# The MLP of a conditioned transformer block: both products as seven block products in place of eight, in groups of 512 tokens, with the first of them among the last steps of cross-attention

## The chip, the cores and the metric

The kernel runs on one core of one Trainium2 chip. The metric is the device time of one execution in microseconds (us), the median of several runs. All arithmetic that matters here is in float32.

## The reference

The block takes 16 images of 224 tokens with 512 channels (3584 tokens), one conditioning vector per image, and 750 context tokens per image. Cut to what matters:

```python
shift_a, scale_a, gate_a, shift_m, scale_m, gate_m = split(silu(c) @ W_mod + b_mod, 6)
x = x + gate_a * proj(self_attention(ln(x) * (1 + scale_a) + shift_a))     # 16 heads of 32
x = x + cproj(cross_attention(ln(x), ln(context)))
x_norm2 = ln(x) * (1 + scale_m) + shift_m
h = gelu(x_norm2 @ W_mlp1 + b_mlp1)        # 512 -> 2048
x = x + gate_m * (h @ W_mlp2 + b_mlp2)     # 2048 -> 512
```

The change is about the last two lines, and about the step that leads into them.

## The kernel before

Three stages follow each other: self-attention in pairs of images, cross-attention image by image, and the MLP. Every instruction is kept in program order on its engine (class `Ordered`, line 19), so the code's order is the order of each queue; since all calls go through that helper, the profile puts them on line 28, and groups are told apart by their tiles.

**A float32 product on TensorE.** A call of `mm` with a stationary block of 128 x 128 and a moving block of 128 x n stands in the profile as two matmul instructions and two weight loads (LDWEIGHTS, shown as engine PEld): each pass streams the n columns once. A transpose (`turn`) is one pass. The text calls one such instruction a *pass*.

**Cross-attention** (from line 698). It goes by units, one for each image b and group g of four heads. `plan` and `at_slot` (line 791) hang the other work of the image (projections, transposes, norms) into six slots of each unit. A unit's `scores` go to the PSUM tile `sc` (four banks, one buffer); VectorE (DVE) keeps a running maximum `top`; ScalarE (ACT) copies the scores to `pt`; one unit later `max_row`, `subtract` (DVE, tile `pt`) and `weights` (exponentials on ACT, the row sums `acc` on GpSimd, POOL) follow, and `values` multiplies with `vt` and adds the sums of `acc` (tile `o`); `finish` divides (DVE, `rinv` and `at`). `project` (line 773) multiplies the heads' results `at` by `wcproj`, adds them to the image `x` (DVE `upd`, then POOL) and writes the image to `x_cross` in DRAM. After the last unit comes a tail written out by hand (lines 993 to 1014): the last unit's weights and values, with four products of the MLP set between them (`ahead`), and the last image's `project`.

**The MLP** (from line 1018) takes four groups of 896 tokens. For a group, `mlp_load` fetches a chunk of 128 tokens (tile `mx`), `mlp_norm` normalises it (statistics on DVE, the rest on POOL), `mlp_turn` transposes it on TensorE and modulates it on DVE into `mxt`. For the first group these steps are hung into the slots of the last image of cross-attention (lines 828 to 837), all seven chunks of them. The first product (`mlp_1`, line 684) makes 128 of the 2048 rows of `h` for 448 tokens from four calls, eight passes of 448 columns; ACT applies the GELU (`h`). The second product then makes 128 tokens x 512 channels from 16 calls, 32 passes of 512 columns; DVE adds the bias (`upd`), POOL multiplies by the gate and adds the image, and the rows go out. While it runs, the next group is loaded, normalised and turned. The four weight blocks of each product are loaded by SyncE's queue (SP), those of the second when the memory of cross-attention has come free.

Of the kernel before, what the change touches and what calls it, by code (L numbers as in the profile page):

```python
# [8 lines left out]
F32 = mybir.dt.float32  # L9
# [28 lines left out]
def kernel(  # L38
# [44 lines left out]
    NG = B // GB  # L83
    GT = GB * N
    GC = GT // P
    HT = GT // 2
    NT = 3
# [64 lines left out]
    x_cross = [dram.tile([GT, H], F32, name=f"x_cross{q}") for q in range(NG)]  # L152
# [269 lines left out]
    def load_cross():  # L422

        mod_pool.close()
        p = cross_weights.enter_context(tc.tile_pool(name="w_cross", bufs=1, side="right"))
# [215 lines left out]

    mlp_in = ExitStack()
    mlp = {}
    mx = {}

    def mlp_begin():
        context_pools.close()
        p = mlp_in.enter_context(tc.tile_pool(name="ml_in", bufs=1, side="right", reuse_waits="tile"))
        mlp["in"] = p
        mlp["w1"] = []  # L650
        mlp_weights(2)

    def mlp_weights(n):
        for i in range(len(mlp["w1"]), n):
            mlp["w1"].append(load_w(mlp["in"], w_mlp1[:, i * H : (i + 1) * H], f"w1_{i}"))

    def mlp_load(i):
        q, c = divmod(i, GC)
        mx[i] = cw["mx"].tile([P, H], F32, name="mx")
        nc.sync.dma_start(out=mx[i], in_=x_cross[q][c * P : (c + 1) * P, :])  # L660

    def mlp_norm(i):
        Norm([mx[i]], [mx[i]], P).all()

    def mlp_turn(psum, i):
        q, c = divmod(i, GC)
        if c == 0:
            mlp["xt"] = [mlp["in"].tile([P, GT], F32, name=f"mxt{k}") for k in range(KC)]
# [4 lines left out]
        lo, hi = c * P, (c + 1) * P  # L673
        while lo < hi:
            b = lo // N
            to = min((b + 1) * N, hi)
            for k in range(KC):
                at = (k - c) * P
                modulate(
                    ps[:, at + lo : at + to], mlp["xt"][k][:, lo:to], q * GB + b, k, i_shift_m, i_scale_m  # L680
                )
            lo = to

    def mlp_1(ps, m, half):
        w, lo = mlp["w1"][m // KC], (m % KC) * P
        for k in range(KC):
            mm(
                ps[:, :HT], w[:, k, lo : lo + P], mlp["xt"][k][:, half * HT : (half + 1) * HT],
                start=(k == 0), stop=(k == KC - 1),
            )  # L690
# [4 lines left out]
    with tc.tile_pool(name="ca", bufs=2, reuse_waits="tile") as ca:  # L695
# [98 lines left out]
        for b in range(B):  # L794
# [30 lines left out]
            if n == B:  # L825
# [6 lines left out]
                at_slot(b, 3, 0, lambda: mlp_weights(MLP // H))  # L832
                for c, (u, slot) in enumerate(((2, 3), (2, 4), (2, 5), (3, 0), (3, 1), (3, 2), (3, 4))):
                    at_slot(b, u, slot, lambda c=c: mlp_turn(ps_mm, c))
                    if 4 + c < GC:
                        at_slot(b, u, slot, lambda c=c: mlp_load(4 + c))
                        at_slot(b, *((2, 5), (3, 0), (3, 1))[c], lambda c=c: mlp_norm(4 + c))
# [155 lines left out]
        early = {}  # L993
        sc = ps_s.tile([P, HG, 512], F32, name="sc")

        def ahead(m):
            early[m, 0] = sc[:, m, :]
            mlp_1(early[m, 0], m, 0)
# [8 lines left out]
        ahead(2)  # L1007
# [10 lines left out]
    with tc.tile_pool(name="ml", bufs=3, reuse_waits="tile") as ml:  # L1018
        hs = {}

        def gelu(ps, m, half):
            if half == 0:
                hs[m] = ml.tile([P, GT], F32, name="h", bufs=NF + 1)
            nc.scalar.activation(
                hs[m][:, half * HT : (half + 1) * HT], ps[:, :HT], AF.Gelu_apprx_tanh,
                bias=bcol[:, o_mlp + m : o_mlp + m + 1],
            )

        for (m, half), ps in early.items():
            gelu(ps, m, half)  # L1030
        attention_psum.close()

        w2 = [load_w(ml, w_mlp2[i * H : (i + 1) * H, :], f"w2_{i}") for i in range(MLP // H)]
        bmlp2 = bias_rows(ml, b_mlp2, P, "bmlp2")
        resid = {}

        def fetch(i):
            if i < NG * GC:
                q, c = divmod(i, GC)
                t = ml.tile([P, H], F32, name="xr")  # L1040
                nc.sync.dma_start(out=t, in_=x_cross[q][c * P : (c + 1) * P, :])
                resid[i] = t, gate_rows(ml, 1, i * P, P)

        fetch(0)
        fetch(1)
        with (
            tc.tile_pool(name="ml_h", bufs=4, space=PSUM, reuse_waits="tile") as ps_h,
            tc.tile_pool(name="ml_mm", bufs=4, space=PSUM, reuse_waits="tile") as ps_mm,
        ):
            for q in range(NG):  # L1050
                for m in range(NF):
                    for half in range(2):
                        if q or (m, half) not in early:
                            ps = ps_h.tile([P, 512], F32, name="h_ps")
                            mlp_1(ps, m, half)
                            gelu(ps, m, half)
                more = q + 1 < NG
                if more:
                    mlp_load((q + 1) * GC)
                    mlp_load((q + 1) * GC + 1)  # L1060
                for c in range(GC):
                    i = q * GC + c
                    if more:
                        if c + 2 < GC:
                            mlp_load(i + GC + 2)
                        mlp_norm(i + GC)
                    ps = ps_mm.tile([P, 512], F32, name="mm")
                    for m in range(NF):
                        mm(
                            ps[:, :H], hs[m][:, c * P : (c + 1) * P], w2[m // KC][:, m % KC, :],  # L1070
                            start=(m == 0), stop=(m == NF - 1),
                        )
                    fetch(i + 2)
                    if more:
                        mlp_turn(ps_mm, i + GC)
                    x_r, gate = resid.pop(i)
                    add_to_x(ml, ps[:, :H], x_r, bmlp2, gate)
                    nc.sync.dma_start(out=out.flatten_outer_dims()[i * P : (i + 1) * P, :], in_=x_r)
# [36 lines left out]
```

## Time and profile before

| what | value |
|---|---|
| median of 3 runs | 3063.89 us (3062.92 to 3065.47) |
| the profiled execution's own time | 3062.88 us |
| its span in the profile | 3061.1 us |
| TensorE busy | 2965.4 us, 97% of the span |
| DVE, ACT, POOL busy | 1618.5, 1129.1, 1251.9 us |
| granted TensorE clock, mean | 0.99 |
| last image's units end, `project` of it begins | 2267.51 us |
| first matmul of the MLP after that | 2285.06 us |
| last matmul ends, last instruction of POOL begins | 3054.64, 3056.85 us |

The time outside of the span is 1.8 us. In a row of the timeline the first number is the start, the second the length of a run of like instructions, "x8" their number, and a bracket at the end the idle time before them with what ended it. Ends of matmuls are modelled: in a row of passes the next begins before the last one's modelled end, so the pace is read from starts.

### The profile page before, as it was taken

To read this page: it belongs to the slowest core of one execution; us is meant where nothing else is said; L and a number is where in the kernel's file an instruction comes from. 1 tells how busy PE (TensorE), PEld (TensorE's weight loads), DVE (VectorE), ACT (ScalarE), POOL (GpSimd) and SP (SyncE) were. 2 spreads that over 40 slices of the span, in tenths; PEclk is the share of its full clock that TensorE was granted. 3 is DMA by queue.
4 is the path that set the end of the run, shared out by engine and by line. 5 is a ranking of instruction groups with operands and counts; after the bars stand their busy time and mean duration, and the time that the engine had idled before them with its cause. 6 is when DMAs were issued, how large, how long until landed. Compare 5 with 4: busy or idle time off the path is not lost.

```text
span 3061.1 us, 44601 instructions
## 1 busy us (share of the span) xinstructions
PE 2965.4 (97%) x18709; PEld 1622.0 (53%) x18709; DVE 1618.5 (53%) x2294; ACT 1129.1 (37%) x1316; POOL 1251.9 (41%) x1624
## 2 busy tenths in 40 slices
PE   8999999998999999999999999999869999999999
PEld 5554454454556555555555655655535444454444
DVE  3555555564577777777777787777740100201100
ACT  1122222221465656656656566566522011020110
POOL 1022222122366766666766766676640210202101
PEclk9999999999999999999999999999989999999999
DMA  5111110101101000001000101100220110201001
GB/s 182 56 31 31 31 31 17 51 10 31 49 27 33 25 23 30 30 26 33 33 23 21 33 23 33 33 23 1 79 91 18 56 41 14 83 0 55 31 11 41
DMA packets 55373, 114.28 MB, mean 37 GB/s; under 512 B 4308, under 2 KB 4372, under 8 KB 55172
## 3 DMA queue, kind: packets, MB, share of 16 engines
q1 hardware_dynamic: 54560, 110.58, 11.2%
q8 instruction: 147, 2.41, 0.3%
q10 hardware_dynamic: 612, 0.85, 0.1%
q14 instruction: 54, 0.44, 0.0%
HBM read 89.33 MB, written 22.09 MB: 36 GB/s over the span
## 4 chain that ended last, share of the span: by engine, by line
PE 73%; issue 12%; DVE 7%; POOL 4%; ACT 3%; DMA 1%; POOLq 0%; ACTq 0%; SPq 0%; DVEq 0%
PE mm L28 50%; PE sc L28 9%; PE o L28 8%; PE h_ps L28 6%; ACT pt L28 3%; DVE top L28 2%; POOL acc L28 1%; DVE rinv L28 1%; DVE stats L28 1%; POOL upd L28 1%; POOL xr L28 1%; DVE mc L28 1%; DVE m L28 1%; ACT kt L28 0%; DVE pt L28 0%
## 5 line engine op out<-in xcount | busy, mean ns | idle before, releaser
L28 POOL TENSOR_TENSOR acc<-acc,pt 125x448 f32<-125x448 f32 x512 | 583.5, 1140 | 40.2
L28 POOL TENSOR_TENSOR upd<-upd,gate 112x512 f32<-112x512 f32 (+1 forms) x60 | 76.1, 1269 | 1124.7 <-DVE upd L28 1120.0
L28 DVE TENSOR_TENSOR pt<-pt,o 125x896 f32<-125x896 f32 x384 | 394.4, 1082 | 91.1 <-PE o L28 86.1
L28 ACT COPY pt<-sc 125x1792 f32<-125x1792 f32 x192 | 317.4, 1653 | 225.7 <-DVE top L28 201.3
L28 PE MATMUL mm<-w,h 128*128 128x512 f32 x896 | 388.2, 592 | 0.0
L28 PE MATMUL h_ps<-mxt,w 128*128 128x448 f32 x992 | 376.3, 542 | 9.2 <-ACT h L28 9.2
L28 DVE TENSOR_TENSOR top<-top,sc 125x896 f32<-125x896 f32 x320 | 346.7, 1083 | 40.6 <-PE sc L28 34.0
L28 PE MATMUL mm<-wkvc,cxt 128*125 128x512 f32 x768 | 354.4, 604 | 8.6 <-ACT kt L28 8.6
L28 PE MATMUL mm<-cxt,wkvc 128*128 128x375 f32 x1024 | 349.9, 484 | 2.5 <-ACT cxt L28 2.5
L28 ACT ACTIVATE pt<-pt 125x896 f32<-125x896 f32 x384 | 339.3, 955 | 14.5 <-DVE pt L28 13.7
L28 DVE TENSOR_SCALAR mxt<-mm,mod_t 128x128 f32<-128x128 f32 (+3 forms) x160 | 47.0, 362 | 510.3 <-PE mm L28 510.3
L28 POOL TENSOR_TENSOR acc<-pt 125x448 f32<-125x448 f32 x128 | 146.2, 1142 | 375.1 <-ACT pt L28 375.1
L28 ACT ACTIVATE h<-h_ps,bcol 128x448 f32<-128x448 f32 x124 | 78.6, 634 | 595.6 <-PE h_ps L28 595.6
L28 PEld LDWEIGHTS h_ps<-mxt,w 128*128 128x128 f32 x992 | 189.3, 191 | 194.4 <-issue 184.4
L28 PEld LDWEIGHTS mm<-w,h 128*128 128x128 f32 x896 | 168.8, 190 | 205.3 <-issue 205.3
L28 DVE RECIPROCAL rinv<-o 128x224 f32<-128x224 f32 x128 | 198.8, 1553 | 115.5 <-PE o L28 115.5
L28 PEld LDWEIGHTS mm<-cxt,wkvc 128*128 128x128 f32 x1024 | 190.1, 191 | 112.6 <-issue 12.9
L28 ACT ACTIVATE pt<-sc 112x1792 f32<-112x1792 f32 x64 | 106.5, 1664 | 362.1 <-PE sc L28 362.1
L28 DVE TENSOR_REDUCE m<-sc 112x8 f32<-112x1792 f32 x64 | 129.7, 2026 | 207.3 <-PE sc L28 207.3
L28 PEld LDWEIGHTS mm<-wkvc,cxt 128*125 128x125 f32 x768 | 136.5, 187 | 175.2 <-issue 153.5
L28 PE MATMUL sc<-qt,kt 32*125 32x224 f32 x3072 | 201.9, 377 | 14.6 <-ACT pt L28 14.1
L28 PE MATMUL mm<-xt,wqkv 128*128 128x448 f32 x512 | 208.9, 551 | 4.7 <-DVE xt L28 4.7
(110 smaller groups left out, 3541.9 us busy)
## 6 DMA issues: line engine op xcount, KB each, us to landing
cx<-in_ctx_dram SPq DMA_DIRECT2D x96, 250.0 KB
w<-in_L_xcond_W_mlp_dram SPq DMA_DIRECT2D x8, 1024.0 KB
x<-in_x_dram SPq DMA_DIRECT2D x16, 448.0 KB
x_self<-x SPq DMA_DIRECT2D x16, 448.0 KB
x<-x_self SPq DMA_DIRECT2D x16, 448.0 KB
x_cross<-x SPq DMA_DIRECT2D x16, 448.0 KB
mx<-x_cross SPq DMA_DIRECT2D x28, 256.0 KB
xr<-x_cross SPq DMA_DIRECT2D x28, 256.0 KB
```

The costliest lines, as they stand in the source:

```text
L28: return lambda *args, **kw: self.tc.keep_in_program_order(f(*args, **kw))
```

## The change

Both products are cut into 2 x 2 blocks and made from seven block products in place of eight (Strassen's scheme, in the form with fifteen sums). Group size goes from 896 to 512 tokens, seven groups in place of four.

**First product.** A weight block of 512 x 512 (`w1[i]`) is one factor, the turned tokens 512 x 512 (`mxt`) the other; each of the seven products of class `First` is four calls, eight passes, of 256 columns. Sums of weight blocks (`ws`, made once by `mlp_sums`) and of token blocks (`tt`, made for each group by `mlp_turned`) are four instructions each with both inputs in SBUF; one of each four overwrites a quarter of its source. The seven results are added up in three PSUM tiles (`a`, `b`, `c`) and three SBUF tiles of `mx`: ACT copies two of them out, DVE copies one and adds three, and ACT makes eight GELUs of 256 columns. Group 0 of block 0 is still made plainly (`mlp_plain`, eight passes of 512 columns each), in the tail of cross-attention where `ahead` stood.

**Second product** (`second`). 256 tokens x 2048 by 2048 x 512; each of the seven products is 8 calls, 16 passes, of 256 columns. The sums of `h` are eight DVE instructions, in place, for each 256 tokens; those of the weights are made once on POOL (`sums_2`). Seven evictions on DVE build `upd`, and POOL closes the rows as before.

**The end of cross-attention.** The tail now also holds, on DVE, the sums of group 0's tokens and of weight block 1; on TensorE, after `values`, the first two products of `First(1)`, then `project` into a tile of its own (`tail`), then the other five. `h0` is allotted in the pool `ml_in`, so the first GELUs don't wait for the memory of cross-attention. In the last image's slots four chunks are turned where seven were. `w1[2]` is loaded into the buffer of `wqc`, `w1[3]` with the second product's weights.

The diff, cut to its core:

```diff
-    GT = GB * N
+    GT = 512
...
+    def combine_right(engine, b11, b12, b21, b22, t1, t2, t3, t4):
+        engine.tensor_tensor(t1, b12, b11, ALU.subtract)
+        engine.tensor_tensor(t3, b22, b12, ALU.subtract)
+        engine.tensor_tensor(t2, b22, t1, ALU.subtract)
+        engine.tensor_tensor(t4, b21, t2, ALU.subtract)
+    def mlp_sums(engine, pool, i):
+        w = mlp["w1"][i]
+        mlp["ws"][i] = ws = pool.tile([P, 3, 2, HT], F32, name=f"ws{i}", bufs=1)
+        lo, hi = w[:, :2], w[:, 2:]
+        combine(engine, lo[:, :, :HT], hi[:, :, :HT], lo[:, :, HT:], hi[:, :, HT:],
+            ws[:, 0], ws[:, 1], lo[:, :, HT:], ws[:, 2])
...
+    class First:
+            self.blocks = {
+                1: (w[:, lo, :HT], xt[:, lo, :HT]), 2: (w[:, hi, :HT], xt[:, hi, :HT]),
+                4: (w[:, hi, HT:], tt[:, 2]), 7: (w[:, lo, HT:], xt[:, lo, HT:]),
+            }
+                self.blocks.update({3: (ws[:, 2], xt[:, hi, HT:]), 5: (ws[:, 0], tt[:, 0]), 6: (ws[:, 1], tt[:, 1])})
+        def begin(self, a, c):
+            self.product(a, 1, True)
+            self.p1 = self.part()
+            nc.scalar.copy(self.p1, a)
+            self.product(c, 2, True)
+            nc.vector.tensor_tensor(self.p1, c, self.p1, ALU.add)
+        def rest(self, b):
+            self.product(a, 6, False)
+            nc.vector.tensor_copy(u2, a)
+            self.product(b, 5, True)
+            nc.scalar.copy(p5, b)
+            self.out(self.p1, 0, 0)
+            self.product(a, 7, False)
+            nc.vector.tensor_tensor(p5, a, p5, ALU.add)
+            self.out(p5, 1, 1)
+            self.product(b, 3, False)
+            nc.vector.tensor_tensor(u2, b, u2, ALU.add)
+            self.out(u2, 0, 1)
+            self.product(a, 4, False)
+            self.out(a, 1, 0)
...
         prev.values()
-        ahead(0)
+        mlp_plain(sc[:, 0], 0)
         cur.max_row()
         prev.finish()
-        ahead(1)
+        mlp_plain(sc[:, 1], 1)
...
         cur.weights(1)
-        ahead(3)
+        mlp_plain(sc[:, 3], 3)
+        mlp_turned(nc.vector)
+        mlp_sums(nc.vector, mlp["in"], 1)
+        for m in range(KC):
+            gelu(sc[:, m], mlp["h"][0][:, m], m)
         cur.values()
         cur.finish()
+        ahead = First(1)
+        ahead.begin(*(ps_mm.tile([P, 512], F32, name="mm") for _ in range(2)))
+        tail = ps_s.tile([P, HG, 512], F32, name="sc")
         for c in range(TC):
-            project(B - 1, c)
+            project(B - 1, c, tail[:, c])
...
+        mlp_weights(ml, "w1_3")
+        ahead.rest(tail[:, 2])
+        mlp_sums(nc.vector, ml, 2)
...
+                product(a, a11, b11, True)
+                for i in range(n):
+                    nc.vector.tensor_tensor(s1[i], a21[i], a22[i], ALU.add)
+                    nc.vector.tensor_tensor(a21[i], a11[i], a21[i], ALU.subtract)
+                evict(0, lo, a)
+                for i in range(n):
+                    nc.vector.tensor_tensor(a11[i], s1[i], a11[i], ALU.subtract)
+                between(1)
+                product(c, a12, b21, True)
+                add(0, lo, c)
+                for i in range(n):
+                    nc.vector.tensor_tensor(a12[i], a12[i], a11[i], ALU.subtract)
+                between(2)
+                product(a, a11, t2, False)
+                evict(0, hi, a)
+                between(6)
+                product(b, s1, t1, True)
+                evict(1, hi, b)
+                between(5)
+                product(a, a21, b12, False)
+                add(1, hi, a)
+                between(7)
+                product(b, a12, b22, False)
+                add(0, hi, b)
+                close(0)
+                between(3)
+                product(a, a22, t4, False)
+                evict(1, lo, a)
+                close(1)
...
+                    first(2)
+                    mlp_sums(nc.vector, ml, 3)
+                    sums_2()
+                    first(3)
+                    mlp_sums(nc.gpsimd, ml, 0)
```

`between` holds the next group's loads, norms and turns; `combine` is the mirror image of `combine_right`.

How the change moves instructions at three places. DVE, at the end of the last image: here is what stands before, from the last unit's maxima to the last `project`.

```order
L28 TENSOR_REDUCE mc<-mm 112x4 x2
L28 RECIPROCAL rinv<-o 128x224
L28 TENSOR_TENSOR at<-o,rinv 128x224
L28 TENSOR_TENSOR pt<-pt,o 125x896 x6
L28 RECIPROCAL rinv<-o 128x224
L28 TENSOR_TENSOR at<-o,rinv 128x224
L28 TENSOR_TENSOR upd<-mm,bcproj 112x512 x2
```

And in the change, from the last `subtract` on (`ws` and the `w` beside it are the sums and the block of `w1[1]`):

```order
L28 TENSOR_TENSOR pt<-pt,o 125x896 x6
L28 TENSOR_TENSOR tt<-mxt 128x512
L28 TENSOR_TENSOR mxt<-mxt 128x2x256
L28 TENSOR_TENSOR tt<-mxt,tt 128x512 x2
L28 TENSOR_TENSOR ws_18006<-w_1_17674 128x512
L28 TENSOR_TENSOR w_1_17674<-w_1_17674 128x2x256
L28 TENSOR_TENSOR ws_18006<-ws_18006,w_1_17674 128x512
L28 TENSOR_TENSOR ws_18006<-w_1_17674,ws_18006 128x512
L28 RECIPROCAL rinv<-o 128x224
L28 TENSOR_TENSOR at<-o,rinv 128x224
L28 TENSOR_TENSOR mx<-mm,mx 128x512
L28 TENSOR_TENSOR upd<-sc,bcproj 112x512 x2
```

Eight instructions with two inputs in SBUF have come between the last `subtract` and the last division.

TensorE at the same place, before: the last unit's values and sums, `project`, and the MLP.

```order
L28 MATMUL o<-pt,vt 32x224 x24
L28 MATMUL o<-acc,ones 32x224 x4
L28 MATMUL mm<-wcproj,at 112x512 x8
L28 MATMUL h_ps<-mxt_17681,w_0_17672 128x448
L28 MATMUL h_ps<-mxt_17682,w_0_17672 128x448
```

In the change (a row's count is of calls, two passes each; `a`, `b`, `c` are the new PSUM tiles):

```order
L28 MATMUL o<-pt,vt 32x224 x24
L28 MATMUL o<-acc,ones 32x224 x4
L28 MATMUL mm<-mxt,w_1_17674 128x256 x8
L28 MATMUL sc<-wcproj,at 112x512 x8
L28 MATMUL mm<-tt,ws_18006 128x256 x4
L28 MATMUL sc<-tt,ws_18006 128x256 x4
L28 MATMUL mm<-mxt,w_1_17674 128x256 x4
L28 MATMUL sc<-mxt,ws_18006 128x256 x4
L28 MATMUL mm<-tt,w_1_17674 128x256 x4
L28 MATMUL a<-mxt,wqc 128x256 x4
```

Two block products have moved ahead of `project`, and products of the MLP stand directly behind it.

POOL, after the last image's sums, before:

```order
L28 TENSOR_TENSOR acc<-acc,pt 125x448 x4
L28 TENSOR_TENSOR x<-x,upd 112x512 x2
L28 TENSOR_TENSOR rstd<-mv,eps 128x1
L28 TENSOR_TENSOR rstd<-rstd,neghalf 128x1
L28 TENSOR_SCALAR nb<-mv,rstd 128x1
```

In the change (the `w` of this piece are blocks of the second product's weights, `wcproj` the buffer that its first sums reuse):

```order
L28 TENSOR_TENSOR acc<-acc,pt 125x448 x4
L28 TENSOR_TENSOR x<-x,upd 112x512 x2
L28 TENSOR_TENSOR wcproj<-w_0_18128 128x4x256
L28 TENSOR_TENSOR w_0_18128<-w_2_18132,w_0_18128 128x4x256
L28 TENSOR_TENSOR wcproj<-w_2_18132,wcproj 128x4x256
L28 TENSOR_TENSOR w2t_0_18198<-w_2_18132,wcproj 128x1024
L28 TENSOR_TENSOR w2t_18203<-w_1_18130 128x4x256
L28 TENSOR_TENSOR w_1_18130<-w_3_18134,w_1_18130 128x4x256
L28 TENSOR_TENSOR w2t_18203<-w_3_18134,w2t_18203 128x4x256
L28 TENSOR_TENSOR w2t_1_18204<-w_3_18134,w2t_18203 128x1024
```

Eight sums of 1024 columns have come in behind the image's last addition (and four of 512 for `w1[0]` after them).

More of the change, by code (lines that the diff above doesn't have):

```diff
@@ L1021, in gelu @@
[L1021 to L1030, printed above, removed]
+        for i in range(1, NW):
+            mlp["h"][i] = ml.tile([P, KC, GT], F32, name=f"h{i}", bufs=1)
@@ L1046 @@
+        def fetch(i):
+            t = ml.tile([P, H], F32, name="xr")
+            q, lo = divmod(i * P, GR)
+            nc.sync.dma_start(out=t, in_=x_cross[q][lo : lo + P, :])
+            resid[i] = t, gate_rows(ml, 1, i * P, P)
         with (
-            tc.tile_pool(name="ml_h", bufs=4, space=PSUM, reuse_waits="tile") as ps_h,
-            tc.tile_pool(name="ml_mm", bufs=4, space=PSUM, reuse_waits="tile") as ps_mm,
-        ):
-            for q in range(NG):
[L1051 to L1078, printed above, removed]
```

184 lines of the change are left out of this document (145 added, 39 removed).

## Prediction

> **What bounds the kernel now.** I read the page's busy times and slices first, then the timeline of the MLP, then the chain that ended last.
>
> ```profile
> span 3061.1 us, 44601 instructions
> PE 2965.4 (97%) x18709; PEld 1622.0 (53%) x18709; DVE 1618.5 (53%) x2294; ACT 1129.1 (37%) x1316; POOL 1251.9 (41%) x1624
> PE   8999999998999999999999999999869999999999
> PE 73%; issue 12%; DVE 7%; POOL 4%; ACT 3%; DMA 1%; POOLq 0%; ACTq 0%; SPq 0%; DVEq 0%
> ```
>
> TensorE is the bound. Its one dip (the slices with 8 and 6) is the end of cross-attention. The MLP is the last quarter:
>
> ```profile
> 2310.00:2400.00 90.00, 90.00 (x235) 43.87 (x234) 2.75 (x7) 13.31 (x21) 4.26 (x6) 1.00 0.04 12
> ...
> 2285.06 25.17 PE L28 MATMUL h_ps<-mxt,w 128*128 128x448 f32 x59 [9.15 <-ACT h L28]
> ...
> 2300.12 0.63 ACT L28 ACTIVATE h<-h_ps,bcol 128x448 f32<-128x448 f32 x1 [2.37 <-PE h_ps L28]
> 2303.12 0.63 ACT L28 ACTIVATE h<-h_ps,bcol 128x448 f32<-128x448 f32 x1 [2.37 <-PE h_ps L28]
> ...
> 3019.71 34.93 PE L28 MATMUL mm<-w,h 128*128 128x512 f32 x81
> ...
> 3041.01 0.69 DVE L28 TENSOR_TENSOR upd<-mm,bmlp 128x512 f32<-128x512 f32 x1 [13.04 <-PE mm L28]
> 3054.74 0.69 DVE L28 TENSOR_TENSOR upd<-mm,bmlp 128x512 f32<-128x512 f32 x1 [13.04 <-PE mm L28]
> ```
>
> There TensorE is busy throughout (90.00 of 90) at a granted clock of 1.00 while DVE, ACT and POOL are nearly idle (2.75, 13.31, 4.26): whatever is taken off TensorE there comes off the time, and the others have room for sums. Evictions stand 3.00 us apart in the first product, so eight passes of 448 columns cost 0.3755 us each; 13.73 us apart in the second, so 32 passes of 512 cost 0.429 each. From 2285.06 to 3019.71 + 34.93 = 3054.64 the stretch is 769.6 us.
>
> **The products (term A).** The change makes more and shorter passes: its gain hangs on what 256 columns cost. The nearest rows are 224 columns, and transposes of 125, each pass with weights of its own:
>
> ```profile
> 1526.79 1.68 PE L28 MATMUL mm<-xt,wqc 128*128 128x224 f32 x8
> 1528.30 1.02 PE L28 MATMUL mm<-ident,top 125*112 125x125 f32 x8
> 1529.25 2.48 PE L28 MATMUL o<-pt,vt 125*32 125x224 f32 x48
> ...
> L28 PEld LDWEIGHTS mm<-w,h 128*128 128x128 f32 x896 | 168.8, 190 | 205.3 <-issue 205.3
> ```
>
> Eight passes of 224 take 1.51 us from start to start, 0.189 each; with 0.3755 at 448 that is 0.833 ns a column and 2 ns a pass, so 256 columns cost 0.2156. A weight load lasts 190 ns, as long as such a pass, yet it does not show: the transposes go at 0.95 / 8 = 0.119. Passes behind `project`: five products of First(1), 40; 26 more blocks (two in group 0, four in each of six groups) of 56, 1456; 14 calls of `second` of 7 x 16, 1568; together 3064, or 660.6 us. The turns of 24 chunks, four passes of 0.119 each, add some 12. 672.6 against 769.6 is **-97.0 us**. Bounds: 0.2133 a pass if a column alone counts (7 us less), 0.228 with the 15 ns by which the transposes lie above their 125 columns (38 us more); 256 is nearest to 224, and I take that row.
>
> Behind each product stands an eviction. Their prices:
>
> ```profile
> L28 ACT COPY pt<-sc 125x1792 f32<-125x1792 f32 x192 | 317.4, 1653 | 225.7 <-DVE top L28 201.3
> L28 ACT ACTIVATE h<-h_ps,bcol 128x448 f32<-128x448 f32 x124 | 78.6, 634 | 595.6 <-PE h_ps L28 595.6
> L28 DVE TENSOR_TENSOR upd<-mm,bmlp 128x512 f32<-128x512 f32 x28 | 19.1, 683 | 186.3 <-PE mm L28 186.3
> L28 DVE TENSOR_TENSOR at<-o,rinv 128x224 f32<-128x224 f32 x128 | 50.1, 392 | 4.4
> ```
>
> By their slopes ACT needs 0.49 us for 256 columns and 0.68 for 512, DVE 0.42 and 0.68. A block of First lasts 56 x 0.2156 = 12.1 us, a product 1.73; ACT has two copies and eight GELUs, 5.3 us, DVE four of 512, 2.7. The order of the products leaves one product between writing a bank and using it again; the tightest is ACT's copy of product 1, which follows two GELUs of the block before: it ends about 2.6 us into the block, and is wanted at 3.45. In `second` a product lasts 3.45 us and DVE has some 9 of 24 us to do. I take these at nothing; what hides them is the product between, and without it each costs its own length.
>
> **The end of cross-attention (terms B to E).** The chain of waits there, and DVE's last `subtract` from the timeline:
>
> ```profile
> 2208.85 1.28 DVE mxt L28 x4
> ...
> 2222.43 0.62 DVE stats L28
> ...
> 2223.25 2.00 DVE mxt L28 x8
> ...
> 2228.24 0.61 DVE stats L28
> ...
> 2245.59 3.20 PE sc L28 x8
> ...
> 2249.19 3.07 PE sc L28 x8
> ...
> 2254.63 1.16 POOL acc L28
> ...
> 2258.30 1.14 POOL acc L28
> ...
> 2265.46 1.14 POOL acc L28
> 2266.64 0.94 PE o L28 x4
> 2267.58 8.34 PE mm L28 x16
> ...
> 2278.08 3.33 DMA x_cross<-x
> ```
>
> ```profile
> 2256.06 3.08 DVE L28 TENSOR_TENSOR pt<-pt,o 125x896 f32<-125x896 f32 x3 [0.50 <-PE o L28]
> ```
>
> B: the 9.15 us before 2285.06 were ACT's GELUs waiting for cross-attention's memory (they follow the write of `x_cross`). `h0` lies elsewhere now and First(1)'s products need none of it: **-9.15**. Next late there is ACT's first GELU into `h1`, which still waits for that write, some 5.5 us behind `project`; TensorE has 8.6 us of products by then, and only their last one's bank is wanted after it.
>
> C: two products of First(1) now stand before `project`: 16 x 0.2156 = +3.45. The plain products stream 512 columns for 448, 8 x 0.0535 = 0.43 more each; two of the four lie on the chain (the rows `sc` at 2245.59 and 2249.19), the others under POOL's sums: +0.86. **+4.3.**
>
> D: three chunks fewer in the last image. On the chain they free the rows from 2208.85 to 2228.24: 1.28 + 0.62 + 2.00 + 0.61, **-4.5** (the turn that moves from 2208.85 goes where ACT's copy covers it; none to all of the 7.5 us of DVE work taken out, 0 to -7).
>
> E: the sums of tokens and of `w1[1]`, eight instructions of 512 columns, follow DVE's `subtract`, which ends at 2259.14. POOL's `acc` then runs to 2266.6, TensorE waiting. Is DVE free beside POOL? The trace has large DVE instructions beside `acc` unharmed, but each reads PSUM with one input. With two inputs in SBUF it has only tiny ones:
>
> ```profile
> 675.56 0.79 POOL L28 TENSOR_SCALAR cx<-cx,rstd,nb 125x512 f32<-125x512 f32 x1
> 675.92 0.45 DVE L28 TENSOR_TENSOR rest<-m,nm 112x8 f32<-112x8 f32 x1
> ...
> L28 DVE TENSOR_TENSOR rest<-m,nm x64: 171/172/445, 53.9 to 730.1; 112x8 f32<-112x8 f32 x64
> ...
> L28 POOL TENSOR_TENSOR xr<-xr,upd 128x512 f32<-128x512 f32 x28 | 35.4, 1264 | 2.2
> L28 POOL TENSOR_TENSOR acc<-acc,pt 125x448 f32<-125x448 f32 x512 | 583.5, 1140 | 40.2
> ```
>
> One of 64, begun 0.36 us into a POOL instruction, took 0.445 us for 0.172 and ended with it (676.37 and 676.35). I read this as the two taking turns. The Trainium skill, SBUF — State Buffer, "Who interferes with whom", says the same: a VectorE instruction with two SBUF inputs contends with GpSimd instructions that read SBUF, and the loser is blocked for the whole instruction; by it the rows of `pt` and `top` are free and the new sums are not. Taking turns, six `acc` instructions are left after 2259.4, each behind one DVE sum: 6 x 0.683 = 4.1 us later. TensorE's idle of 4.5 us (2262.1 to 2266.64) grows to 8.6 and its clock drops for longer: after 4.5 us sixteen passes took 8.34 for 6.9, after 9.15 us the first 59 took 25.17 for 22.2; I add the difference, 1.5. **+5.6** (0 to 7).
>
> **Weights and the steady run (terms F, G).** The loads move at this rate:
>
> ```profile
> 2285.00:2290.00 5.00, 4.94 (x7) 2.49 (x8) 0.00 (x0) 0.01 (x1) 0.00 (x0) 0.50 1.01 352
> ```
>
> F: a block of 1.05 MB takes 3 us. Counted from `project`'s end (2275.9 before), the write of `x_cross` ends at +5.5, `w1[3]` lands at +8.5, the four of the second product at +11.5 to +20.4. POOL's sums of 1024 columns cost 2.26 each by the slope from 448 to 512; from +17.5 they run without a gap, past +33. First(2) ends on TensorE at 8.6 + 12.1 = +20.7, and DVE begins the four sums of `w1[3]` at +19.8, each behind a POOL sum: the third, which product 6 of First(3) reads, ends at +28.7 where product 6 wants it at +24.1; the fourth and two evictions make product 7 wait 0.8 more. **+5.5** (0, if they don't take turns or `w2` lands late, to 4 x 2.26 = 9). The weights themselves are in time: the third product of `second` at +44 wants POOL's seventh sum, done by +36.
>
> G: in the second half of each group, DVE's first four sums of `h` meet POOL's last norm and its closing of the 256 tokens before (2 x 1.264). Taking turns, the in-place sums that product 3 reads come out about 0.5 us late: 7 x 0.5, **+3.5** (0 to 14). The last eviction is 256 wide, -0.3.
>
> Sum: -97.0 - 9.15 + 4.3 - 4.5 + 5.6 + 5.5 + 3.5 - 0.3 = -92.0. The profiled execution's own time is 3062.88 (span 3061.1 and 1.8 around it), 1.0 below the median; -92.0 on the median 3063.89 is **2972**.
>
> **The rivals.**
> 1. DVE and POOL don't take turns. For it: it is one row in 64, and others took 0.17 beside POOL, as here, where POOL had begun 0.06 us before (and may not yet have read):
>
> ```profile
> 250.38 0.80 POOL L28 TENSOR_SCALAR xn<-x,rstd,nb 112x512 f32<-112x512 f32 x1
> 250.44 0.17 DVE L28 TENSOR_TENSOR rest<-m,nm 112x8 f32<-112x8 f32 x1
> ```
>
> E, F and G go: 2957.
> 2. The evictions become the bound: TensorE waits at every block because ACT, strictly in order, copies product 1 behind GELUs that themselves wait for DVE. Against it: 5.3 of 12.1 us. At 1 us in each of 26 blocks and 14 halves it gives 2972 + 40 = 3012.
> 3. Slower: weight loads come out from behind the shorter passes. The Trainium skill, TensorE: Matmul & The Clock Gate, "The mechanism", says that a load overlaps with running matmuls only for another row group; here all use the whole array, so by it every pass would pay. By rows, the load is 190 ns: 3064 x 0.190 = +582, 3554; it decides from 92 / 3064 = 30 ns a pass. Against it: the 224-column row, whose loads are of that kind and cost 2 ns; the trace does not bear this rule out.
>
> **Chances.** Forecast 0.63, rival 1 0.17, rival 2 0.17, rival 3 0.03. The forecast's own bounds (D, E, F, G; a pace of 0.228 would land beside rival 2 and is left out with it) make 2957 to 2987; rival 1 sits at the lower end, and D can take 2 more: 2955 to 2988, with most of rival 2 and rival 3 left out. About 0.2% of the time, 6 us, can be told from no change. All but rival 3 are faster by far: 0.96; within 0.2% 0.01; slower 0.03.
>
> **What would show it.** Right: rows of 256 columns at 0.215 to 0.217 a pass, TensorE full in the MLP, DVE rows of two SBUF inputs longer than 0.68 where POOL runs, `acc` ending 4 us later against the last `subtract`, a gap of 4 to 6 us before product 6 of First(3). Wrong: gaps before each product (rival 2), a pace near 0.25 or above (rival 3), sums at 0.68 throughout (rival 1). A saving of under 75 us would mean that a wait stands in the steady run that I have not seen.

## The result, and the profile after

| what | before | after |
|---|---|---|
| median | 3063.89 us (3062.92 to 3065.47, 3 runs) | 2966.99 us (2962.8 to 2967.63, 4 runs) |
| the profiled execution's own time, its span | 3062.88, 3061.1 us | 2967.63, 2965.8 us |
| TensorE busy | 2965.4 us, 97% | 2877.7 us, 97% |

The ratio is 0.968 (95% interval 0.9664 to 0.9697): the changed kernel is faster by some 97 us. The forecast was 2972 us, in a range of 2955 to 2988.

The page of the changed kernel, lines of its busy times and its slices:

```profile
span 2965.8 us, 47584 instructions
...
PE 2877.7 (97%) x19901; PEld 1851.1 (62%) x19901; DVE 1843.2 (62%) x2624; ACT 1175.4 (40%) x1462; POOL 1289.0 (43%) x1636
...
PE   8999999999999999999999999999988999999999
```

TensorE is still the bound, and is busy for the same 97% of a shorter span. Its dip at the end of cross-attention is shallower (slices of 8 and 8 where 8 and 6 stood). TensorE has 1192 more instructions and 87.7 us less work; DVE has taken up 224.7 us more without becoming the bound.

The MLP in the windows of the changed kernel (time, then busy us of PE, PEld, DVE, ACT, POOL, the granted clock, DMA); the second window is the whole stretch from the first product behind `project` to the last eviction:

```profile
2370.00:2470.00 100.00, 100.00 (x473) 88.05 (x472) 41.99 (x83) 18.52 (x40) 19.06 (x26) 1.00 0.14 43
2282.24:2959.74 677.50, 673.69 (x3161) 592.21 (x3159) 290.57 (x534) 124.39 (x269) 146.53 (x163) 1.00 0.16 51
```

TensorE is full, as before, with DVE at 42% where it had 3%. Over the whole stretch TensorE lacks 3.8 us of 677.5, and that is one wait. The rows of the changed kernel's timeline give the pace and that wait:

```profile
2304.07 2.83 POOL L28 TENSOR_TENSOR wcproj<-w,wcproj 128x1024 f32<-128x1024 f32 x1
2304.70 2.75 DVE L28 TENSOR_TENSOR w<-w 128x512 f32<-128x512 f32 x1
...
2307.37 2.82 DVE L28 TENSOR_TENSOR ws<-ws,w 128x512 f32<-128x512 f32 x1
2310.34 3.38 PE L28 MATMUL a<-tt,ws 128*128 128x256 f32 x8 [3.76 <-DVE ws L28]
2313.56 1.89 PE L28 MATMUL b<-tt,ws 128*128 128x256 f32 x8
...
2320.47 3.62 PE L28 MATMUL a<-w,h 128*128 128x256 f32 x16
2323.92 3.62 PE L28 MATMUL c<-w,h 128*128 128x256 f32 x16
```

A product of 16 passes begins 3.45 us after the one before it: 0.2156 us a pass. Ahead of product 6 of First(3) stands the wait for `ws`: DVE's sums of `w1[3]` take 2.8 us each beside POOL's sums of 1024 columns. The eight passes behind the wait take 3.22 us for 1.73, at a granted clock of 0.55.

The end of cross-attention in the changed kernel's timeline:

```profile
2259.84 1.45 DVE L28 TENSOR_TENSOR mxt<-mxt 128x512 f32<-128x512 f32 x1
2261.21 3.16 DVE L28 TENSOR_TENSOR tt<-mxt,tt 128x512 f32<-128x512 f32 x2
...
2262.36 6.06 POOL L28 TENSOR_TENSOR acc<-acc,pt 125x448 f32<-125x448 f32 x4
...
2268.48 0.96 PE L28 MATMUL o<-acc,ones 125*32 125x224 f32 x4 [6.46 <-POOL acc L28]
...
2269.37 5.13 PE L28 MATMUL mm<-mxt,w 128*128 128x256 f32 x16
...
2274.34 3.60 PE L28 MATMUL sc<-wcproj,at 128*112 128x512 f32 x8
...
2278.72 3.69 PE L28 MATMUL sc<-wcproj,at 128*112 128x512 f32 x8 [0.78 <-DVE upd L28]
...
2282.24 1.89 PE L28 MATMUL mm<-tt,ws 128*128 128x256 f32 x8
```

The sums of tokens and of `w1[1]` take 1.45 to 1.6 us each while `acc` runs (only the first 0.88), not 0.68, and POOL's `acc` 1.52 each, not 1.14; TensorE waits 6.46 us where it waited 4.51. The hole of 9.15 us behind `project` is gone. A wait of 0.78 has come up inside `project`, which the forecast didn't have.

**Where the time went.** The same seven stretches of the two profiled executions, by the starts of the rows at their ends:

| stretch, up to | before | after | difference | forecast |
|---|---|---|---|---|
| the first product of the context's keys and values | 759.28 | 765.00 | +5.72 | 0 |
| the last image's anchor (a `subtract` of DVE, 2200.12 and 2205.71) | 1440.84 | 1440.71 | -0.13 | 0 |
| the last unit's first `subtract` (2252.48, 2252.23) | 52.36 | 46.52 | -5.84 | D and the plain products, -3.64 |
| TensorE's sums of `acc` (2266.64, 2268.48) | 14.16 | 16.25 | +2.09 | E without the clock, +4.1 |
| the first product of the MLP behind `project` (2285.06, 2282.24) | 18.42 | 13.76 | -4.66 | B, two products, clock: -4.2 |
| the last eviction's start (3054.74, 2959.74) | 769.68 | 677.50 | -92.18 | A, F, G: -88.0 |
| the end of the span | 6.36 | 6.06 | -0.30 | -0.3 |
| sum | | | -95.3 | -92.0 |

The first stretch runs the same instructions in both kernels. Its 5.7 us go with a lower clock between 50 and 100 us; the window of before, then that of after:

```profile
50.00:100.00 50.00, 49.46 (x396) 28.48 (x394) 28.90 (x59) 8.21 (x7) 5.90 (x12) 0.93 0.24 81
```

```profile
50.00:100.00 50.00, 50.00 (x364) 27.81 (x363) 24.43 (x51) 7.54 (x6) 5.91 (x12) 0.86 0.17 53
```

At 0.86 for 0.93 TensorE issues 364 instructions where it issued 396. Counted from that first product on, which takes such differences out, the kernel before needs 2301.8 us and the changed one 2200.8: 101.0 less. The experiments below are counted so too; a *profile total* in them is the time from that product to the end of the span.

### The profile page after: what moved, and what is told of

Its sections match the earlier page's. It is cut to its first block, busy times and chain, and to the rows that moved or that the text cites. A ratio compares the mean times of both kernels' runs of the same rounds, so it can differ in the third digit from the quotient of the medians.

```text
span 2965.8 us, 47584 instructions
## 1 busy us (share of the span) xinstructions
PE 2877.7 (97%) x19901; PEld 1851.1 (62%) x19901; DVE 1843.2 (62%) x2624; ACT 1175.4 (40%) x1462; POOL 1289.0 (43%) x1636
## 4 chain that ended last, share of the span: by engine, by line
PE 81%; DVE 7%; issue 4%; ACT 3%; POOL 3%; DMA 1%; SPq 0%; ACTq 0%; POOLq 0%; DVEq 0%
PE mm L28 46%; PE a L28 10%; PE sc L28 9%; PE o L28 9%; PE b L28 5%; ACT pt L28 3%; PE c L28 3%; DVE top L28 1%; POOL acc L28 1%; DVE rinv L28 1%; DVE stats L28 1%; DVE mc L28 1%; DVE m L28 1%; ACT kt L28 1%; POOL upd L28 0%
## 5 line engine op out<-in xcount | busy, mean ns | idle before, releaser
L28 POOL TENSOR_TENSOR rstd<-mv,eps 112x2 f32<-112x2 f32 (+3 forms) x93 | 18.0, 194 | 475.7 <-DVE mv L28 475.7
L28 PEld LDWEIGHTS sc<-qt,kt 32*125 32x125 f32 x3072 | 134.0, 184 | 92.9 <-issue 41.2
L28 ACT COPY mrow<-mm 128x896 bf16<-128x896 bf16 x64 | 58.0, 906 | 309.5 <-PE mm L28 309.5
L28 PE MATMUL o<-pt,vt 125*32 125x224 f32 x3072 | 158.5, 354 | 0.0
L28 PEld LDWEIGHTS mm<-xt,wqkv 128*128 128x128 f32 x512 | 92.5, 191 | 86.8 <-issue 81.0
L28 ACT COPY mx<-a 128x512 f32<-128x512 f32 x26 | 15.2, 586 | 325.1 <-POOL upd L28 306.3
```

The costliest lines, as they stand in the source:

```text
L28: return lambda *args, **kw: self.tc.keep_in_program_order(f(*args, **kw))
```

## The experiments

The first theory throughout is that of the prediction: the gain is the passes, and DVE and POOL get in each other's way where both of a DVE instruction's inputs lie in SBUF. Each ratio is against the kernel before, run beside it on the same chip (medians of 3063.5 to 3067.8 us).

### The change again

> The change once more, nothing altered. In the first profile of the change everything ahead of the last image lay 5.6 us later than before the change, though the program is the same up to there. If that is chance (the clock in the first 100 us), the first product of cross-attention starts somewhere from 759 to 766 us and the total moves with it, 2962 to 2968. If the change itself costs it, it starts at 765 again and the total is 2967.

Measured 2966.24 us (2962.93 to 2968.43, 4 runs), ratio 0.9677 (0.9661 to 0.9693). In the profiled execution the first product of keys and values stood at 759.87 for 765.00, with a clock of 0.93 between 50 and 100 us as in the kernel before, and the rest took 2201.3 us. So the 5.7 us of the first stretch are no part of the change, and its worth in a profile is 100.5 to 101.0 us.

### The sums of w1[3] ahead of First(2)

```diff
-                    first(2)
                     mlp_sums(nc.vector, ml, 3)
+                    first(2)
```

> The four DVE sums of w1[3] come ahead of First(2), when POOL is idle, and not behind it, beside POOL's sums of the second product's weights. Taking turns: each lasts 0.69 us in place of 2.6 to 2.8, the wait of 3.8 us before product 6 of First(3) and the slow clock behind it (1.5) go, 5 us in all: about 2962. If the long rows came from the weights having just landed, or from TensorE reading beside them, they stay over 2 us, and the wait moves into First(2): 2967 or more.

Measured 2964.39 us (2960.3 to 2965.33), ratio 0.9666 (0.9651 to 0.968). From the first product behind `project` to the last eviction it took 674.57 us for 677.50. The sums took 0.69 us each and the wait of 3.76 was gone, but another had come, so that the profile total fell to 2197.9 us: 3 to 3.5 us of the 5 that were expected; in this kernel's timeline, in the first half of group 0's second product:

```profile
2321.48 0.41 DVE L28 TENSOR_TENSOR upd<-a,bmlp 128x256 f32<-128x256 f32 x1
2321.81 3.08 DVE L28 TENSOR_TENSOR h<-s,h 128x512 f32<-128x512 f32 x2
2322.76 1.59 POOL L28 TENSOR_TENSOR ws<-w,ws 128x512 f32<-128x512 f32 x1
...
2323.37 1.97 PE L28 MATMUL a<-wcproj,h 128*128 128x256 f32 x8 [2.27 <-DVE h L28]
```

TensorE now came 5.4 us earlier to the second product, while POOL was still at its sums (the last two of the second product's weights, then those of `w1[0]`), and the third product of that half waited for DVE's sums of `h`. The eviction beside them, with one input in PSUM, took its usual 0.41. Term F's cause holds; the wait that followed it had been hidden by it.

### The sums of tokens and of w1[1] behind the last division

```diff
-        mlp_turned(nc.vector)
-        mlp_sums(nc.vector, mlp["in"], 1)
         for m in range(KC):
...
         cur.finish()
+        mlp_turned(nc.vector)
+        mlp_sums(nc.vector, mlp["in"], 1)
         ahead = First(1)
```

> The eight DVE sums of group 0's tokens and of w1[1] come behind the last division and not ahead of it, so POOL's row sums of the last unit run alone. Taking turns: the last five acc come at 1.19 us a piece in place of 1.5, TensorE's wait before the sums shrinks from 6.5 us to about 4.5, and the total falls by 2 to 3 us: about 2964.5. Without turns nothing moves there, and the sums, later, could only cost: 2967 to 2969.

Measured 2966.25 us (2962.54 to 2967.23), ratio 0.9672 (0.9658 to 0.9687). Its timeline:

```profile
2260.66 4.75 POOL L28 TENSOR_TENSOR acc<-acc,pt 125x448 f32<-125x448 f32 x4
2265.46 0.96 PE L28 MATMUL o<-acc,ones 125*32 125x224 f32 x4 [4.38 <-POOL acc L28]
2266.35 6.11 PE L28 MATMUL mm<-mxt,w 128*128 128x256 f32 x16
2272.30 3.60 PE L28 MATMUL sc<-wcproj,at 128*112 128x512 f32 x8
```

POOL's four `acc` took 4.75 us for 6.06 and TensorE waited 2.08 less, as the turns would have it. The two products behind took 5.95 us for 4.97, at a granted clock of 0.59 for 0.71, so half of it was given back. The profile total is 2200.0 us, 0.8 to 1.4 less than in the two profiles of the change, and the median is that of the change repeated: the fall of 2 to 3 us that was expected did not come.

### The second input of these sums from PSUM

```diff
-        mlp_turned(nc.vector)
-        mlp_sums(nc.vector, mlp["in"], 1)
+        mlp_turned(nc.vector, sc)
+        mlp_sums(nc.vector, mlp["in"], 1, sc)
...
+    def one_from_psum(engine, sc, outs, ins):
+        for j, (o, i) in enumerate(zip(outs, ins)):
+            engine.tensor_tensor(o, i, sc[:, j].rearrange("p (k t) -> p k t", k=2), ALU.add)
```

The eight instructions keep their place, number and size. Since they add what lies in `sc`, they are not the scheme's sums.

> As the change, but the second input of the same eight DVE instructions, same place and size, is read from PSUM (banks of the plain products) and not from SBUF; the numbers that they make are not the sums that the scheme needs. If two inputs in SBUF are what meets POOL: DVE 0.69 us each for 1.5, acc at 1.19, the wait 2 us shorter. If any DVE instruction that writes SBUF at that place slows POOL (its writes, or what ACT and TensorE read there): as in the change, 1.5 us each and a wait of 6.5.

One run, 2967.18 us. Its timeline:

```profile
2260.23 0.69 DVE L28 TENSOR_TENSOR mxt<-mxt,sc 128x512 f32<-128x512 f32 x1
2261.82 4.75 POOL L28 TENSOR_TENSOR acc<-acc,pt 125x448 f32<-125x448 f32 x4
...
2266.62 0.96 PE L28 MATMUL o<-acc,ones 125*32 125x224 f32 x4 [4.38 <-POOL acc L28]
```

Here both engines run at their own pace side by side: 0.69 for 1.45 to 1.6, and 1.19 a piece for `acc`. What makes them wait for each other is the second input in SBUF, not the mere company. That is rival 1 refuted. The two products behind took 6.05 us for 4.97, so that half of the 2.08 us was given back here too.

### The second product plain

```diff
-                    sums_2()
...
+                for j in range(2):
+                    for m in range(NF):
+                        mm(ps[:, :H], mlp["h"][m // KC][:, m % KC, at : at + P], w2[m // KC][:, m % KC, :],
+                            start=(m == 0), stop=(m == NF - 1))
+                    nc.vector.tensor_tensor(upd[j], ps[:, :H], bmlp2, ALU.add)
```

> The first product by seven block products, the second plain again (32 passes of 512 columns for 128 tokens); the sums of h and POOL's sums of the second product's weights go. Theory (the gain is the passes alone, and the wait of 3.8 us before product 6 of First(3) is VectorE meeting POOL's sums): 14 halves take 2 x 13.73 = 27.46 us for 24.15, +46.4; without POOL's sums the wait and the low clock behind it go, -5.3; with the changed kernel at 2966 that is 3007. Rival 1 (the wait comes from something else, such as the arrival of the weights): it stays, 3012. Rival 2 (the block products cost waits of their own, so that the second product saves less than its passes): under 3002.

Measured 3008.27 us (3004.09 to 3008.65), ratio 0.9814 (0.9798 to 0.983). From the first product of keys and values on it took 2241.9 us, 40.6 to 41.1 more than the changed kernel; the theory had 46.4 - 5.3 = 41.1. In its timeline the same place of First(3), without POOL's sums of the second product's weights:

```profile
2301.95 0.68 DVE L28 TENSOR_TENSOR ws<-w 128x512 f32<-128x512 f32 x1
2302.66 0.69 DVE L28 TENSOR_TENSOR w<-w 128x512 f32<-128x512 f32 x1
...
2306.31 1.89 PE L28 MATMUL a<-tt,ws 128*128 128x256 f32 x8
```

The sums stand where they stood, take 0.69 us each, and product 6 doesn't wait. So POOL's sums were the cause of F, not the arrival of the weights.

### Both products plain

```diff
-                f = First(i)
-                f.begin(bank("a"), bank("c"))
-                f.rest(bank("b"))
+                for m in range(KC):
+                    ps = bank("abca"[m])
+                    mlp_plain(ps, i * KC + m)
+                    gelu(ps[:, :GT], mlp["h"][i][:, m], i * KC + m)
```

> Both products plain, but the groups of 512 tokens, the earlier h0, the four chunks in the last image's slots, the sums in the tail and the two products of First(1) ahead of project stay (First(1) of group 0 keeps its seven products). The tokens of group 0 are read by blocks 2 and 3 with a quarter overwritten by the sums, and block 1 of the weights is loaded again, so these values are not the reference's. Theory: 26 blocks at 13.73 us for 12.07, +43 on the kernel with only the second product plain, 3050; the rest, some 14 to 17 us below the kernel before, is what the end of cross-attention gave. Rival (the new end of cross-attention gives nothing, and all comes from the passes): 3064 to 3068, as the kernel before.

Measured 3050.16 us (3045.95 to 3051.54), ratio 0.9953 (0.9938 to 0.9968). From the first product of keys and values on it took 2284.5 us: 42.6 more than with only the second product plain (theory 43), and 17.4 less than the kernel before. The gain of 101 thus divides into 42.6 from the first product, some 41 from the second (the 46.4 of its passes less term F), and 17.4 from all the rest, in which First(1) of group 0, still in seven products, has some 1.7 (13.73 - 12.07).

### The tail in another order

```diff
         prev.values()
-        mlp_plain(sc[:, 0], 0)
         cur.max_row()
         prev.finish()
-        mlp_plain(sc[:, 1], 1)
+        mlp_plain(sc[:, 0], 0)
...
-        cur.values()
+        cur.values(lambda: mlp_plain(sc[:, 3], 3))
+        gelu(sc[:, 3], mlp["h"][0][:, 3], 3)
...
-            project(B - 1, c, tail[:, c])
+            project(B - 1, c, tail[:, c] if c else None)
```

Both moved sums are in it as well.

> The sums of w1[3] ahead of First(2), the sums of tokens and of w1[1] behind the last division, the fourth plain product between the last values and the sums of acc, the running maximum's last steps ahead of the first plain product, and the first chunk of project in a PSUM tile of its own. From the first product of the context's keys to the end the changed kernel takes 2201, with the sums of w1[3] early 2198. Theory (the plain products stand on the chain that leads to POOL's acc, and TensorE's 4.4 us of waiting behind them can hold one): one plain product (3.4) comes off the chain, the wait of 0.8 in project goes, 1.1 from the sums behind: 2192 to 2193. Rival (POOL's acc starts no earlier, only the clock stays higher): 2196 to 2197, the wait before the sums of acc about 1 us.

Measured 2954.26 us (2953.05 to 2954.55), ratio 0.9641 (0.9627 to 0.9656). From the first product of keys and values on it took 2192.4 us, as the theory said; the rival is out, since the last unit's first `acc` begins 2.6 us earlier, too (1486.7 us behind that product, for 1489.3 with only the sums of `w1[3]` moved). But the number is in part luck. Up to the first product behind `project` the gain over that kernel is 7.1 us where the theory had 5.3, and behind it 1.7 are lost again, since the passes behind the wait of the third product took 3.33 us here and 1.80 there. Its timeline:

```profile
2255.88 3.70 PE L28 MATMUL sc<-mxt,w 128*128 128x512 f32 x8 [1.47 <-ACT h L28]
...
2259.51 0.58 PE L28 MATMUL o<-acc,ones 125*32 125x224 f32 x8
...
2260.03 3.72 PE L28 MATMUL mm<-mxt,w 128*128 128x256 f32 x16
...
2263.59 3.60 PE L28 MATMUL mm<-wcproj,at 128*112 128x512 f32 x8
...
2267.02 3.60 PE L28 MATMUL sc<-wcproj,at 128*112 128x512 f32 x8
...
2312.74 3.49 PE L28 MATMUL a<-wcproj,h 128*128 128x256 f32 x8 [2.41 <-DVE h L28]
2316.07 1.89 PE L28 MATMUL a<-w2t,h 128*128 128x256 f32 x8
```

A plain product fills the wait for `acc` (ahead of it 1.47 us are left, for ACT's GELUs), and with the shorter idle the 16 passes behind take 3.56 us, near the 3.45 of full pace, for 4.97 and 5.95. The wait in `project` is gone with the first chunk in a PSUM tile of its own, so that wait came from the two chunks' sharing one tile; it stood at 0.78 us in the run that moved only the sums. The wait before the third product of `second` is left.

### And POOL's sums of w1[0] later

```diff
-                    mlp_sums(nc.gpsimd, ml, 0)
...
                     second(q, half, lambda p, half=half: between(half, p))
+                    if (q, half) == (0, 0):
+                        mlp_sums(nc.gpsimd, ml, 0)
```

> The same as the kernel sent beside it with the other order of the tail, and POOL's sums of w1[0] moved behind the first half of group 0's second product. With the sums of w1[3] early a wait of 2.3 us had come up before the third product of the first half. Theory (VectorE's first sums of h meet POOL's sums of w1[0]): the wait goes, 2 to 2.5 us less than the kernel beside it between the first product behind project and the last eviction. Rival (they meet POOL's sums of the second product's weights, which run that long): the wait stays at 2 us or more.

Measured 2951.4 us (2949.79 to 2955.41), ratio 0.9635 (0.962 to 0.9649): with an interval that lies under that of the change repeated. It overlaps that of the kernel with the other order of the tail, so what this step alone is worth is read from the profiles. The window from the first product behind `project` to the last eviction:

```profile
2269.61:2941.90 672.29, 672.25 (x3161) 591.60 (x3159) 285.59 (x533) 124.28 (x269) 145.08 (x163) 1.00 0.16 51
```

The wait is gone, and the stretch took 3.9 us less than in the kernel with the other order alone (676.23): 2.41 of wait and 1.60 of slow passes behind it (3.33 us for 1.73), which the expectation had left out. The first two of DVE's sums of `h` still stood beside POOL's sums of the second product's weights (2.12 and 2.72 us), as the rival had it, but the next ran at 0.64 to 0.69, and that was enough. TensorE now never waits in the MLP: 672.25 busy of 672.29.

### Seven chunks in the last image's slots again

```diff
-                for c, (u, slot) in enumerate(((2, 4), (2, 5), (3, 1), (3, 2))):
+                for c, (u, slot) in enumerate(((2, 3), (2, 4), (2, 5), (3, 0), (3, 1), (3, 2), (3, 4))):
-                    at_slot(b, u, slot, lambda c=c: mlp_turn(ps_mm, c))
+                    at_slot(b, u, slot, lambda c=c: mlp_turn(ps_mm, c, mlp["h"][0] if c >= GC else None))
+                    if c < 3:
+                        at_slot(b, u, slot, lambda c=c: mlp_load(4 + c))
+                        at_slot(b, *((2, 5), (3, 0), (3, 1))[c], lambda c=c: mlp_norm(4 + c))
```

> The changed kernel with all seven chunks loaded, normalised and turned in the last image's slots again, as in the kernel before; the three extra ones are modulated into the tile that later takes the first GELUs, and made again for group 1, so nothing that is computed changes. From the last image's anchor (VectorE's first subtraction of the row maxima, behind the bf16 product o<-mrow) to the start of the last unit's first subtraction the changed kernel takes 46.5 us. First theory (the rows of the prediction alone: 1.28, 0.62, 2.00, 0.61): 51.0, and 4.5 us on the whole. Rival (as the two traces of before and after suggest: besides these rows the last turn ahead of the transposed maxima, 0.4, and a lower clock over the eight passes of project behind a longer wait, 0.7, and more): 53.0 to 53.4, 6.5 to 6.9 on the whole.

Measured 2970.6 us (2968.71 to 2974.74), ratio 0.9692 (0.9676 to 0.9708). The stretch from the anchor took 53.27 us for 46.52, +6.75, and the profile total is 2207.8 us, 6.5 to 7.0 more than in the two profiles of the change: the rival. The medians lie only 3.6 to 4.4 us apart; they hold the first stretch as well, which took 759.12 us here for 765.00 and 759.87. Its timeline at the image's last `project`, and that of the changed kernel behind it:

```profile
2233.93 1.87 PE L28 MATMUL sc<-qt,kt 32*125 32x224 f32 x16 [5.31 <-ACT pt L28]
2235.73 5.40 PE L28 MATMUL mm<-wcproj,at 128*112 128x512 f32 x8
2240.97 0.60 PE L28 MATMUL mm<-ident,mx 128*128 128x128 f32 x4
2241.41 1.15 PE L28 MATMUL mm<-ident,top 125*112 125x125 f32 x8
```

```profile
2234.53 1.76 PE L28 MATMUL sc<-qt,kt 32*125 32x224 f32 x16 [3.12 <-ACT pt L28]
2236.22 4.62 PE L28 MATMUL mm<-wcproj,at 128*112 128x512 f32 x8
2240.68 1.02 PE L28 MATMUL mm<-ident,top 125*112 125x125 f32 x8
```

With the chunks TensorE waits 5.31 us for 3.12, the eight passes behind take 5.24 for 4.46, and a turn of 0.44 stands ahead of `mm<-ident,top`. These two things, 1.2 us, were in none of the rows that the forecast added up.

## Why the prediction was right, step by step

The mechanism was right, and the median of 2967 lies 5 us below the forecast. Counted without the start-up it is more: 101 us measured for 92 forecast. That the median lies so near is in part luck, since the slower start of the profiled execution hides some of it. The large term, A, came out to 0.1%; the miss is in the small ones. The 9 us of it are 2.2 in D, 2.0 in E's turns and 1.25 in its clock, 3.5 in G and some 0.6 in A and F, less the 0.78 of a wait that was not foreseen.

- **A, right.** 672.6 us forecast for the products and turns; 672.29 where no wait is left in them. The pace of 0.2156 us, worked out from the rows of 224 and 448 columns, is the measured one, and the two plain kernels bear it out (42.6 us measured for 43, 40.6 to 41.1 for 41.1). The weight loads of 190 ns, as long as nine tenths of a pass, stay hidden (rival 3): 592 us of loads lie under 674 of matmuls. By the rule of the Trainium skill, TensorE: Matmul & The Clock Gate, "The mechanism", as the forecast read it, each of these loads would have shown; for float32 blocks of 128 x 128 the trace doesn't agree. The same section also lets loads into a background weight buffer run ahead, which the forecast left out; the trace does not show whether these were such.
- **B, right.** The hole of 9.15 is gone, and nothing took its place there: ACT's first GELUs of 512 columns no longer wait for the write of the image.
- **C, right in passes.** The plain products cost +0.86 by position: the last image is 6.70 us ahead of before at the first of them, and 5.84 behind the second. The two products of First(1) took 4.97 us for 3.45, but `project` behind them regained what the clock had cost it before (two chunks in 7.12 us without the new wait, for 8.39), so the extra clock is 1.52 - 1.27 = +0.25, not +1.5. The 0.78 in `project` was unforeseen: `tail` is one PSUM tile, so the second chunk waited until DVE had read the first.
- **D, mis-sized.** -6.7 for -4.5. The four rows of DVE that were added up are in it, but they are not the whole chain. A `subtract` stands between the third row and the fourth; here it is before, then in the change:

```profile
2225.16 3.08 DVE L28 TENSOR_TENSOR pt<-pt,o 125x896 f32<-125x896 f32 x3
```

```profile
2226.25 3.07 DVE L28 TENSOR_TENSOR pt<-pt,o 125x896 f32<-125x896 f32 x3
```

Counted from the anchor it comes 4.5 us earlier in the change, where the three rows ahead of it make 3.9. The second norm, the fourth row with its aggregate, brings the gap to 5.3; the slower clock behind a longer wait and one more turn on the chain add 1.2, and small steps 0.2.

- **E, mis-sized.** +2.1 for +4.1. That they hinder each other is shown; that each `acc` stands behind a whole DVE sum is not what happened. An `acc` of 448 columns grew by some 0.33 us (1.19 to 1.52 with the step between them), not by 0.68. The Trainium skill, SBUF — State Buffer, "Who interferes with whom", names the pair of instructions rightly and says that one in PSUM is free, which the run with PSUM shows; but it has the loser blocked for the whole instruction of the other, and by that, counted as in the forecast, 4.1 us would have come.
- **F, right.** 3.76 us of wait and 1.49 of slow passes, 5.25, for 5.5. DVE's sums took 2.62 to 2.82 each, so they did stand behind POOL's. Moving these sums alone did not bring it all back, since a wait of 2.3 showed behind; with POOL's sums of `w1[0]` moved too, neither is left.
- **G, wrong.** Forecast +3.5, measured 0: in none of the 14 halves does TensorE wait. The rows of one steady half:

```profile
2446.32 1.75 DVE L28 TENSOR_TENSOR s<-h,h 128x512 f32<-128x512 f32 x1
...
2447.60 1.59 POOL L28 TENSOR_TENSOR xr<-xr,upd 128x512 f32<-128x512 f32 x1
2448.10 1.64 DVE L28 TENSOR_TENSOR h<-h 128x512 f32<-128x512 f32 x1
...
2450.00 1.28 DVE L28 TENSOR_TENSOR h<-s,h 128x512 f32<-128x512 f32 x2
2450.90 0.60 PE L28 MATMUL mm<-ident,mx 128*128 128x128 f32 x4
...
2451.33 1.89 PE L28 MATMUL a<-wcproj,h 128*128 128x256 f32 x8
```

The clash is there: 1.6 to 1.75 us for a sum of 0.69. But the first in-place sum that product 3, the third of the half, reads is ready about 2450.65, half of 1.28 behind 2450.00, and product 3 begins at 2451.33 behind a turn. There are 0.7 us to spare where the forecast had it 0.5 late. Of the four sums ahead of it only two stood beside the closing for their whole length; the first ran at 0.68 and the second took 1.15. The forecast gives 0.5 without a sum, so it can't be said which part of it was too large.

Rival 2 (evictions) is out: DVE and ACT are busy for 42 and 19 of 100 us, and no block waits.

## What to carry to other kernels

Fewer and shorter passes on the bounding engine can be priced from two rows of different width before the change is written, and the price held to 0.1%. A sum on DVE with both inputs in SBUF ran at its own pace only while POOL was not at work in SBUF: look up what POOL does at that time and whether anything waits for the sum, or give the sum an input in PSUM, and put one-time sums where nothing waits for them. When a wait is removed, ask which wait it had been hiding, and count the slow passes behind a wait as part of it.

## What the runs showed of the hardware

- **Who loses by a clash.** A DVE sum of 512 columns (0.69 us alone) took 1.45 to 1.75 beside POOL instructions of 448 or 512 columns and 2.62 to 2.82 beside those of 1024; it took less where only a part of it met one (0.88, 1.15). POOL's instruction grew by about the same 0.3 to 0.5 whatever its length (448 columns: 1.19 to 1.52; 512: 1.27 to 1.59 and 1.71; 1024: 2.36 to 2.67 and 2.83). So DVE waited for most of POOL's instruction, POOL for only about half of DVE's. What in the instructions makes the difference was not tried.
- **The clock behind a wait.** 4.38 us of waiting were followed by 16 passes in 5.95 and 6.05 us, 6.45 us by 4.97 to 5.09 (six profiles), each for 3.45 at full pace: a shorter wait, and a slower stretch behind it. With 2.41 us eight passes took 3.33 us, with 2.27 us 1.80, for 1.73. Shortening a wait by 2.1 us thus gained only about 1.0 here. Where a product filled it, the 16 passes behind took 3.56 us. What sets the length of the slow stretch was not tried.
